# A fused perceiver layer: gather reads first on the SyncE queue, k and v sums ahead of one merged block transpose, maxima over pairs of score banks, and the join of key blocks two at a time

## The chip, the cores and the metric

The kernel runs on one core of one Trainium2 chip. The metric is the device time of one execution in microseconds (us), as the median of several runs.

## The reference, cut to what matters

Sixteen sequences of 128 rows and width 512 pass three sublayers, each with a layer norm before it and a residual sum after it.

```
x = x + xattn(layernorm(x), ctx)   # 16 heads of 32; 2048 context rows per sequence; softmax over them
x = x + mamba_mlp(layernorm(x))    # in_proj, conv, scan over 128 rows with 16 states, out_proj; rmsnorm; MLP of 2048, gelu
x = x + moe(layernorm(x))          # gates by softmax, two largest; a shared and an expert matrix; bias
```

In the attention, k and v are products of the context with weights (512 x 512), scores are q k, and `softmax(scores) v` is made over 2048 context rows.

## The kernel before, in words

**Steps.** Attention is cut into units: a sequence `b` (16), a block `sb` of 512 context rows (4) and a group `hg` of four heads (4), which makes 256 units (`NU`). The loop over `u` (L1329) makes one unit per step; while `u < 256` a step is called live. The scan of the second sublayer runs 54 steps behind (two sequences at a time, 32 steps for a pair), so that from u = 54 to u = 255 both run in one step, and the pattern of a step's other work repeats every 32 steps. After the live steps the MLP and the experts are fed in (L1346); some of that work falls in the last live steps.

**One live step**, in the order in which it is written: loads (L1337 to L1352); four score products into four PSUM banks, one for each head (L307); the weighted sums of the unit before (L386, `weighted`); the reads of the gather (L348, `gathered`); maxima (L315) on DVE; two products for k or v into `pa` and `pc` (L244, `x_products`); four exponentials on ACT (L325); products of dx with B on POOL (L696); the first scan (L731, with L734 and L710); the block transposes (L338, `blocks`); ACT's copy of `pa` (L285, `hold`); k or v sums on DVE (L264, L274, `x_sums`); PE's transposes of two heads (L358) and their copies (L360); the second scan; then the work of the lists `middle`, `late`, `behind`, `after`, `inner`; and last the other products for k or v (`y_products`, L244) with their sums. Every engine runs its own instructions strictly in this written order (`manual_schedule`, L120).

**Two ways to turn probabilities.** The sum over context rows needs the probabilities with these rows on partitions. For the first two heads of a unit PE transposes (L358). For the other two (`ND = 2`) DVE transposes blocks of 32 x 32 (L338), the result is written to DRAM (L342, `trd`) and read back in four pieces in the right order (L348, `pd`). There is one `pd` buffer. The reads for unit u - 1 are issued in step u, behind `weighted`, and used in step u + 1 (L386 with `pd`).

**k and v sums.** k and v are made by a scheme with seven products of quarters, not eight. In steps with phase 1 (u % 4 = 0 and 2) `y_products` adds to `pc` and must wait until `x_sums` has read it. In steps with u % 4 = 3 the product for dt (L663, in list `behind`) writes `pc` and so waits for the v sum too; its result is read by ACT (L667) and DVE (L670).

**Joining key blocks.** Each block of 512 rows has its own maximum and sum. When a sequence is done (e = 16b + 16), `joined`, `joined_first`, `shares`, `joined_second` and `joined_third` make a factor for each block; `spread_out` (L497, POOL) widens it, `scaled` (L503, L508, L510, then L511 on POOL) turns it, multiplies and adds; `attended` (step e + 6, L516) is the output product. In the kernel before, `spread_out` for blocks 0, 1 and 2, 3 is put at e + 2, e + 3, e + 3, e + 4, and `scaled` one step later each.

**Loads.** All these loads go through SyncE's queue, which issues in the written order and waits in place. `load_bc` (L645) brings B (tile `bc0`, used by L696) two steps ahead and C (tile `bc16`, used by L734) one step ahead, each with two buffers. Context (L158) comes four steps ahead. The weights wq (L171), wo (L173), win (L548) and wout (L553) share a ring of six buffers (`WS`); a load into it waits until PE has used the tile that was there. Two of the eight wout tiles are issued inside the product that uses them (`projected`, L760).

**PSUM.** Four score banks, `avp` (weighted sums), `hst` (scan state), `pa` and `pc`. Work in the list `late` takes score banks 2 and 3 while the first two hold the transposes.

Of the kernel before, what the change touches and what calls it, by code (L numbers as in the profile page):

```python
# [15 lines left out]
P = 128  # L16
# [20 lines left out]
def perceiver_layer(ctx: ExitStack, tc: tile.TileContext, a: dict, out: bass.AP):  # L37
# [75 lines left out]
    with ExitStack() as es:  # L113
# [12 lines left out]

        banks = [psum.tile([P, 512], FP, tag=f"s{j}", name=f"bank{j}") for j in range(4)]
        avp = psum.tile([P, 4, P], FP, tag="av", name="avp")  # L130
        hst = psum.tile([P, NH // 2, GT], FP, tag="h0", name="hst")
        pa = psum.tile([P, 2, 256], FP, tag="pa", name="pa")
# [178 lines left out]

        def maxima(u):
            b, sb, hg = split(u)
            for j in range(4):
                nc.vector.tensor_reduce(  # L315
                    stats[b][0][j][:, sb, hg : hg + 1], banks[j], AX.X, ALU.max, negate=True
                )

        def exps(u):
            b, sb, hg = split(u)  # L320
            nm, sm = stats[b]
            pr = pool.tile([P, 4, 512], FP, tag="pr", name=f"pr{u}", bufs=1)
            for j in range(4):
                h = hg * 4 + j
                nc.scalar.activation(  # L325
                    pr[:, j, :],
                    banks[j],
                    AF.Exp,
                    bias=nm[j][:, sb, hg : hg + 1],
                    accum_out=sm[:, sb, h : h + 1],  # L330
                )
            prs[u] = pr

        def blocks(u):

            t = pool.tile([P, 4, ND, 4, 32], FP, tag="tr", name=f"tr{u}", bufs=1)
            for h in range(ND):
                nc.vector.transpose(  # L338
                    t[:, :, h].rearrange("p c i q -> p i c q"),
                    prs[u][:, NP + h, :].rearrange("p (i c k) -> p i c k", i=4, c=4),  # L340
                )
            nc.sync.dma_start(trd[u % 2], t.rearrange("p c h i q -> p (c h i q)"))  # L342

        def gathered(u):
# [70 lines left out]
        def normal(b):  # L415

            x = xts[b]
            root_third(rstd[:, b : b + 1], *xts.pop((b, "r")))
            xn = keep.tile([P, D], FP, tag="aT", name="xn", bufs=1)
            nc.vector.tensor_scalar(  # L420
                xn, x, mv[:, b, 0:1], rstd[:, b : b + 1], ALU.subtract, ALU.mult
            )
            if b:
                nc.gpsimd.tensor_tensor(x, x, bo, ALU.add)
            xts[b, "n"] = xn
            nm = [keep.tile([P, SB, 4], FP, tag=f"nm{j}", name=f"nm{b}_{j}") for j in range(4)]
            sm = keep.tile([P, SB, H], FP, tag="sm", name=f"sm{b}")
            stats[b] = nm, sm

# [31 lines left out]
        def joined(b):  # L461

            parts, sm = stats[b]
            nm = keep.tile([P, SB, H], FP, tag="nm", name=f"nm{b}")
            for j in range(4):
                nc.vector.tensor_copy(
                    nm.rearrange("p s (k j) -> p s k j", j=4)[:, :, :, j], parts[j]
                )
            stats[b] = nm, sm

# [729 lines left out]


        early = {}
        late, after, inner, middle, loads, head, behind, between = ({} for _ in range(8))

        def put(where, u, f):
            where.setdefault(u, []).append(f)
# [1 line left out]
        for b in range(B):  # L1208
            s = 16 * b
            if b:  # L1210
                put(loads, s - 8, lambda b=b: load_x(b))
                put(loads, s - 5, lambda b=b: load_w(0, b))
                put(inner, s - 8, lambda b=b: moments_of(b))
                put(middle, s - 7, lambda b=b: root_of(b))
                put(inner, s - 7, lambda b=b: normal(b))
                put(late, s - 4, lambda ps, b=b: queries(b, ps))
            e = s + 16
            put(loads, e + 5, lambda b=b: load_w(3, b))
            put(inner, e - 1, lambda b=b: joined(b))
            put(inner, e, lambda b=b: joined_first(b))  # L1220
            put(middle, e + 1, lambda b=b: shares(b))
            put(inner, e + 1, lambda b=b: joined_second(b))
            put(head, e + 2, lambda b=b: joined_third(b))
            for sb in range(SB):
                put(inner, e + 2 + (sb + 1) // 2, lambda b=b, sb=sb: spread_out(b, sb))
                put(late, e + 3 + (sb + 1) // 2, lambda ps, b=b, sb=sb: scaled(b, sb, ps))
            put(late, e + 6, lambda ps, b=b: attended(b, ps))
            put(middle, e + 7, lambda b=b: root_of(b))
            put(inner, e + 7, lambda b=b: normed(b))
            put(late, e + 8, lambda ps, b=b: z_turned(b, ps))  # L1230
        for g in range(NG):
            p = 32 * (g + 1)
            for ec in range(EC):
                put(loads, p + 8 + ec, lambda g=g, ec=ec: load_win(g, ec))
                put(loads, p + 8 + ec, lambda g=g, ec=ec: load_win(g, EC + ec))
                put(late, p + 9 + ec, lambda ps, g=g, ec=ec: x_part(g, ec, ps))
                put(late, p + 9 + ec, lambda ps, g=g, ec=ec: z_part(g, ec, ps))
                put(after, p + 10 + ec, lambda g=g, ec=ec: silu_first(g, ec, xas))
                put(after, p + Z_GATES[ec], lambda g=g, ec=ec: silu_first(g, ec, zss))
# [6 lines left out]
                put(between, s - 1 + 4 * ec, lambda g=g, ec=ec: dt_third(g, ec))  # L1246
            for i in range(GB):
                for ec in range(WS):
                    put(loads, s + 32 + 2 * i, lambda g=g, i=i, ec=ec: load_wout(g, i, ec))
                put(loads, s + 31 + 2 * i, lambda b=g * GB + i: reload_x(b))  # L1250
                put(late, s + 33 + 2 * i, lambda ps, g=g, i=i: projected(g, i, ps))

# [76 lines left out]
        for u in range(last):  # L1329
# [4 lines left out]
            made, phase = divmod(u + 3, 4)  # L1334
            makes = 0 < made < B * SB
            of, phase = ("k", "v")[phase // 2], phase % 2
            load_bc(u + 2 - 32 - LAG, 0)  # L1337
            if u % 4 == 1 and made + 1 < B * SB:
                load_ctx(made + 1, ("c00", "c10", "c11"))
            if u % 4 == 2 and made + 1 < B * SB:  # L1340
                load_ctx(made + 1, ("c01",))
            for f in loads.get(u, ()):
                f()
            if scans and u <= NU:
                decays(g, r, 0)
            if u > NU:  # L1346
# [2 lines left out]
                    fed += 1  # L1349
                if scans:  # L1350
                    decays(g, r, 0)
            load_bc(u + 1 - 32 - LAG, DS)  # L1352
            if u == NU + 1:
                load_rows()
            if live:
# [1 line left out]
            if 1 <= u <= NU:  # L1357
# [2 lines left out]
                    weighted_last(u - 2)  # L1360
                weighted_out(u - 1)
                gathered(u - 1)
            for f in early.get(u, ()):
                f()
            if u == NU:
# [25 lines left out]
            silu_third()  # L1391
            if scans:
                scan(g, r, 0)
            if live:
                blocks(u)
            if live and u % 4 == 2:
                values_kept(u // 4)
            if makes:
# [2 lines left out]
                decays(g, r, 1)  # L1401
            if makes:
                x_sums(of, made, phase, pa, pc)

# [8 lines left out]

            ahead = live and u % 16 in (3, 10) and len(after_turns) == 1
            if ahead:
                after_turns[0](banks[3])
                after_turns, places = (), ()
            if live:  # L1420
                for j in range(NP):
# [10 lines left out]
                    f(ps)  # L1432
                    give_back(ps)
            for f in behind.get(u, ()):
                ps = flat(pc) if makes else banks[2] if live else bank()
                f(ps)
                if not live:
                    give_back(ps)
# [84 lines left out]
```

## Time and profile before

| | us |
|---|---|
| median of 3 runs (3809.18 to 3819.37) | 3809.51 |
| the profiled execution | 3817.92 |
| its span, first to last instruction | 3816.1 |
| PE (TensorE) busy | 3602.9 |
| DVE (VectorE) busy | 2862.3 |
| ACT (ScalarE) busy | 2304.2 |
| POOL (GpSimd) busy | 2139.1 |

The groups of instructions that the change touches, from the page's fifth part and the groups by line:

| line, engine | what | count | busy us | mean ns |
|---|---|---|---|---|
| L315 DVE | maxima, 128x512 from PSUM | 1024 | 635.7 | 680 |
| L338 DVE | block transposes, 128x512 | 512 | 338.8 | 696 |
| L325 ACT | exponentials, 128x512 | 1024 | 688.5 | 684 |
| L264 DVE | k sums, 128x256 | 384 | 164.0 | |
| L274 DVE | v sums, 128x512 | 189 | 126.3 | |
| L516 PE | output product of attention | 128 | 65.4 | 659 |

Median time from issue to landing: 5.4 us for `bc`, 3.0 for `trd`, 3.9 for `pd`, 5.7 for wq and wo, 5.2 for win, 4.5 for wout. In all 816.84 MB move, a mean of 214 GB/s.

How to read the views. Busy time is the union of an engine's instructions. The list of waits gives who sat idle, what ended the wait, and three numbers: the total in us, how often, and the longest. A line of the timeline gives start and length in us, engine, line, operation, output and inputs, the count of merged instructions, and in brackets idle time before it with what ended it. "SPq" is SyncE's queue. Matmuls are pipelined and their ends are modelled. An engine's idle time costs something only where that engine holds up the end.

### The profile page before, as it was taken

Reading aid. Unit: us, or ns where it says so; the run is one execution under the profiler, and the core shown is the slowest. Engines: PE = TensorE matmul, PEld = TensorE weight load, DVE = VectorE, ACT = ScalarE, POOL = GpSimd, SP = SyncE. Lnnn points to the kernel's source line nnn. Section 1 sums busy time; section 2 is a strip of 40 time slices with the busy share of each in tenths; the row PEclk is TensorE's granted clock in tenths of the full one; section 3 lists DMA queues with packets and bytes.
Section 4 is the critical chain, followed back from the end, with each engine's and each line's share of the span. In section 5 each row is a group of like instructions: output and inputs, shape, how many; then the busy total and the mean of one; then the engine's idle time right before and its main releaser. Section 6 shows DMA issues by size and latency. Waiting matters only on the chain. (4 is left out here: it accounts for less than half of the span.)

```text
span 3816.1 us, 69166 instructions
## 1 busy us (share of the span) xinstructions
PE 3602.9 (94%) x24072; PEld 2678.4 (70%) x24072; DVE 2862.3 (75%) x5158; ACT 2304.2 (60%) x5672; POOL 2139.1 (56%) x2097
## 2 busy tenths in 40 slices
PE   8999999999899999999999989998999989999999
PEld 6777777777676767677677767686777666655655
DVE  4555557887788778888697878877887777778843
ACT  3555556777566666667576757675766666545431
POOL 2121115676667566767576666666675657577820
PEclk9999999999999999999999999999999999999999
DMA  4444546776777667676766777767776688677752
GB/s 150 145 157 150 158 139 216 223 229 214 243 226 233 206 217 244 217 235 208 241 220 216 221 251 222 235 212 234 238 238 202 214 245 317 208 270 253 242 188 83
DMA packets 527547, 816.84 MB, mean 214 GB/s; under 512 B 44848, under 2 KB 378960, under 8 KB 526944
## 3 DMA queue, kind: packets, MB, share of 16 engines
q1 hardware_dynamic: 526752, 811.79, 66.6%
q8 instruction: 192, 3.15, 0.3%
q14 instruction: 155, 1.27, 0.1%
q0 software_dynamic: 448, 0.63, 0.1%
HBM read 661.51 MB, written 150.73 MB: 213 GB/s over the span
## 5 line engine op out<-in xcount | busy, mean ns | idle before, releaser
L315 DVE TENSOR_REDUCE nm<-bank 128x1 f32<-128x512 f32 x1024 | 635.7, 680 | 221.4 <-PE bank L307 220.2
L747 POOL TENSOR_TENSOR ysum<-ysum,w 128x512 f32<-128x512 f32 x384 | 499.8, 1302 | 515.6 <-DVE hst L710 324.6
L325 ACT ACTIVATE pr<-bank,nm 128x512 f32<-128x512 f32 x1024 | 688.5, 684 | 68.2 <-DVE nm L315 62.1
L696 POOL TENSOR_TENSOR w<-dx,bc 128x512 f32<-128x512 f32 x512 | 651.6, 1294 | 8.9
L731 DVE TENSOR_TENSOR_SCAN hst<-hst,w 128x512 f32<-128x512 f32 x459 | 560.1, 1220 | 43.8 <-ACT hst L717 41.3
L717 ACT ACTIVATE hst<-dt,alog 128x254 f32<-128x254 f32 x918 | 439.9, 479 | 87.5 <-DVE hst L710 67.8
L338 DVE STREAM_TRANSPOSE tr<-pr 128x512 f32<-128x512 f32 x512 | 338.8, 696 | 85.3 <-ACT pr L325 75.9
L386 PEld LDWEIGHTS avp<-pT,v 128*32 128x32 f32 x4096 | 207.7, 112 | 196.2 <-issue 194.2
L734 DVE TENSOR_TENSOR w<-hst,bc 128x512 f32<-128x512 f32 x459 | 317.2, 691 | 19.3 <-DMA bc<-bcd 3.5
L307 PE MATMUL bank<-kt,qT 32*128 32x512 f32 x2048 | 308.6, 641 | 8.1 <-DVE avs L510 5.4
L360 ACT COPY pT<-bank 128x512 f32<-128x512 f32 x512 | 272.0, 582 | 56.1 <-PE bank L358 56.1
L236 POOL TENSOR_TENSOR t<-c,c 128x512 f32<-128x512 f32 x128 | 163.3, 1276 | 229.6 <-PE pc L244 223.9
L386 PE MATMUL avp<-pT,v 128*32 128x128 f32 x4096 | 288.4, 282 | 1.2 <-ACT pT L360 1.1
L386 PE MATMUL avp<-pd,v 128*32 128x128 f32 x3072 | 215.9, 285 | 57.0 <-DMA pd<-trd 57.0
L358 PE MATMUL bank<-ident,pr 128*128 128x128 f32 x2048 | 265.7, 273 | 0.8 <-ACT pr L325 0.7
L358 PEld LDWEIGHTS bank<-ident,pr 128*128 128x128 f32 x2048 | 238.8, 141 | 25.3 <-ACT pr L325 1.8
L244 PE MATMUL pa<-vs,t 128*128 128x256 f32 x1008 | 254.5, 397 | 0.0
L244 PE MATMUL pa<-t,ks 128*128 128x256 f32 x1024 | 249.1, 386 | 0.0
L575 PE MATMUL bank<-zT,win 128*128 128x256 f32 x992 | 224.8, 379 | 0.0
L244 PEld LDWEIGHTS pa<-vs,t 128*128 128x128 f32 x1008 | 192.3, 197 | 38.5 <-issue 12.6
L262 ACT ACTIVATE kt<-pa,bk 128x256 f32<-128x256 f32 x128 | 53.6, 470 | 263.7 <-PE pa L244 263.7
L244 PEld LDWEIGHTS pa<-t,ks 128*128 128x128 f32 x1024 | 186.5, 190 | 36.7 <-issue 14.7
(313 smaller groups left out, 7556.6 us busy)
## 6 DMA issues: line engine op xcount, KB each, us to landing
bc<-bcd SPq DMA_DIRECT2D x512, 512.0 KB, 5.4
trd<-tr SPq DMA_DIRECT2D x256, 512.0 KB, 3.0
pd<-trd SPq DMA_DIRECT2D x1024, 128.0 KB, 3.9
c<-in_ctxT_dram SPq DMA_DIRECT2D x256, 256.0 KB, 5.1
wf<-in_w_dram SPq DMA_DIRECT2D x124, 512.0 KB, 6.5
wqo<-in_wqkvo_dram SPq DMA_DIRECT2D x128, 256.0 KB, 5.7
win<-in_win_dram SPq DMA_DIRECT2D x128, 256.0 KB, 5.2
wout<-in_wout_dram SPq DMA_DIRECT2D x128, 256.0 KB, 4.5
```

The costliest lines, as they stand in the source:

```text
L244: nc.tensor.matmul(ps[:, r, :], l[:, kc, r * P : (r + 1) * P], m[:, kc, :], start=(i in (1, 2, 5) and r == 0 and kc == 0), stop=(r == 1 an ...
L307: nc.tensor.matmul(banks[j], qts[b][rows, hg, :], kts[u // 4, hg][rows, :], start=True, stop=True)
L315: nc.vector.tensor_reduce(stats[b][0][j][:, sb, hg : hg + 1], banks[j], AX.X, ALU.max, negate=True)
L325: nc.scalar.activation(pr[:, j, :], banks[j], AF.Exp, bias=nm[j][:, sb, hg : hg + 1], accum_out=sm[:, sb, h : h + 1],)
L338: nc.vector.transpose(t[:, :, h].rearrange("p c i q -> p i c q"), prs[u][:, NP + h, :].rearrange("p (i c k) -> p i c k", i=4, c=4),)
L358: nc.tensor.transpose(ps[:, i, :], prs[u][:, j, i * P : (i + 1) * P], ident)
L386: nc.tensor.matmul(avp[j * HD : (j + 1) * HD, v % 4, :], values(v, i, j), pts[v, j][:, i, :] if j < NP else pds[v][:, :, j - NP, i, :], st ...
L696: nc.gpsimd.tensor_tensor(w, dx.unsqueeze(1).to_broadcast([P, NH // 2, GT]), bcs[g * 32 + r, 0][:, i * NH // 2 : (i + 1) * NH // 2, :], AL ...
L717: nc.scalar.activation(bt(h[:, k, :])[:, :, 1:], bt(dt)[:, :, 1:], AF.Exp, scale=aneg[:, ec, n : n + 1],)
L731: nc.vector.tensor_tensor_scan(flat, flat, w.rearrange("p n t -> p (n t)"), 0.0, ALU.mult, ALU.add)
L734: nc.vector.tensor_tensor(w, h, bcs[g * 32 + r, DS][:, i * NH // 2 : (i + 1) * NH // 2, :], ALU.mult)
L747: nc.gpsimd.tensor_tensor(s, s, w, ALU.add)
```

## The change

Six edits in the live steps:

- The loads of a live step (except u = 0) move from the head of the step to a place behind the reads of the gather. Within them the order becomes: the other loads, `bc0`, `bc16`, context.
- The loads of wq, wo, win and wout form a list of their own, `weights`. In live steps they are issued behind `blocks` and its write; later they go with the other loads.
- `blocks` moves behind `x_sums` and makes one transpose instruction for both heads.
- The four score banks become two tiles of two banks each. One reduction gives the negated maxima of two banks; what joins them afterwards makes two copies in place of four.
- `spread_out` for the four blocks goes to e + 2, e + 2, e + 3, e + 3, with `scaled` one step later.
- dt's product takes a free score bank (2 or 3) where `late` leaves one; the piece of late work that is done ahead of PE's transposes takes bank 2 in place of bank 3.

```diff
-        banks = [psum.tile([P, 512], FP, tag=f"s{j}", name=f"bank{j}") for j in range(4)]
+        pairs = [psum.tile([P, 2, 512], FP, tag=f"s{m}", name=f"bank{m}") for m in range(2)]
+        banks = [pairs[j // 2][:, j % 2, :] for j in range(4)]
...
-            for j in range(4):
+            for m in range(2):
                 nc.vector.tensor_reduce(
-                    stats[b][0][j][:, sb, hg : hg + 1], banks[j], AX.X, ALU.max, negate=True
+                    stats[b][0][m][:, sb, hg, :], pairs[m], AX.X, ALU.max, negate=True
                 )
...
-                    bias=nm[j][:, sb, hg : hg + 1],
+                    bias=nm[j // 2][:, sb, hg, j % 2 : j % 2 + 1],
...
-            for h in range(ND):
-                nc.vector.transpose(
-                    t[:, :, h].rearrange("p c i q -> p i c q"),
-                    prs[u][:, NP + h, :].rearrange("p (i c k) -> p i c k", i=4, c=4),
-                )
+            nc.vector.transpose(
+                t.rearrange("p c h i q -> p (h i) c q"),
+                prs[u][:, NP:, :].rearrange("p h (i c k) -> p (h i) c k", i=4, c=4),
+            )
...
-            for j in range(4):
+            for m in range(2):
                 nc.vector.tensor_copy(
-                    nm.rearrange("p s (k j) -> p s k j", j=4)[:, :, :, j], parts[j]
+                    nm.rearrange("p s (k m j) -> p s k m j", m=2, j=2)[:, :, :, m, :], parts[m]
                 )
...
-                put(loads, s - 5, lambda b=b: load_w(0, b))
+                put(weights, s - 5, lambda b=b: load_w(0, b))
...
-            put(loads, e + 5, lambda b=b: load_w(3, b))
+            put(weights, e + 5, lambda b=b: load_w(3, b))
...
-                put(inner, e + 2 + (sb + 1) // 2, lambda b=b, sb=sb: spread_out(b, sb))
-                put(late, e + 3 + (sb + 1) // 2, lambda ps, b=b, sb=sb: scaled(b, sb, ps))
+                put(inner, e + 2 + sb // 2, lambda b=b, sb=sb: spread_out(b, sb))
+                put(late, e + 3 + sb // 2, lambda ps, b=b, sb=sb: scaled(b, sb, ps))
...
-                put(loads, p + 8 + ec, lambda g=g, ec=ec: load_win(g, ec))
-                put(loads, p + 8 + ec, lambda g=g, ec=ec: load_win(g, EC + ec))
+                put(weights, p + 8 + ec, lambda g=g, ec=ec: load_win(g, ec))
+                put(weights, p + 8 + ec, lambda g=g, ec=ec: load_win(g, EC + ec))
...
-                    put(loads, s + 32 + 2 * i, lambda g=g, i=i, ec=ec: load_wout(g, i, ec))
+                    put(weights, s + 32 + 2 * i, lambda g=g, i=i, ec=ec: load_wout(g, i, ec))
...
-            load_bc(u + 2 - 32 - LAG, 0)
-            if u % 4 == 1 and made + 1 < B * SB:
-                load_ctx(made + 1, ("c00", "c10", "c11"))
-            if u % 4 == 2 and made + 1 < B * SB:
-                load_ctx(made + 1, ("c01",))
-            for f in loads.get(u, ()):
-                f()
+
+            def step_loads():
+                for f in loads.get(u, ()):
+                    f()
+                for f in weights.get(u, ()) if u > NU else ():
+                    f()
+                load_bc(u + 2 - 32 - LAG, 0)
+                load_bc(u + 1 - 32 - LAG, DS)
+                if u % 4 == 1 and made + 1 < B * SB:
+                    load_ctx(made + 1, ("c00", "c10", "c11"))
+                if u % 4 == 2 and made + 1 < B * SB:
+                    load_ctx(made + 1, ("c01",))
+
+            if not 1 <= u <= NU:
+                step_loads()
...
-            load_bc(u + 1 - 32 - LAG, DS)
...
                 gathered(u - 1)
+                step_loads()
...
-            if live:
-                blocks(u)
             if live and u % 4 == 2:
                 values_kept(u // 4)
...
                 x_sums(of, made, phase, pa, pc)
+            if live:
+                blocks(u)
+            for f in weights.get(u, ()) if u <= NU else ():
+                f()
...
-                after_turns[0](banks[3])
+                after_turns[0](free[0])
...
-                ps = flat(pc) if makes else banks[2] if live else bank()
+                n = len(late.get(u, ()))
+                if live and n < len(free):
+                    ps = free[n]
+                else:
+                    ps = flat(pc) if makes else banks[2] if live else bank()
```

## The prediction

> **What bounds the kernel now.** I read the page's first part, then the table of 100 us stretches, then TensorE's waits, then the SyncE queue's own waits, then one step of the timeline. The first part:
>
> ```profile
> PE 3602.9 (94%) x24072; PEld 2678.4 (70%) x24072; DVE 2862.3 (75%) x5158; ACT 2304.2 (60%) x5672; POOL 2139.1 (56%) x2097
> ```
>
> The reader is to see that TensorE (PE) is idle for only 3816.1 - 3602.9 = 213 us, so nothing that keeps PE's work as it is can gain more. The table of stretches says where: the 26 stretches from 600 to 3200 us, in which attention and scan run together, hold 180 us of it. PE's waits name it:
>
> ```profile
> PE avp L386 <- DMA pd<-trd: 65.1, 21, 4.8
> PE bank L516 <- POOL aT L511: 34.0, 13, 2.8
> PE pc L244 <- DVE kt L264: 30.5, 25, 2.5
> PE pc L663 <- DVE v L274: 22.9, 32, 0.9
> PE pc L244 <- DVE v L274: 12.9, 24, 1.0
> PE bank L307 <- DVE avs L510: 5.4, 12, 0.5
> ```
>
> (us in total, times, longest.) Six waits, 170.8 us, most of the idle time; each is met by one part of the change. The first is the gather of the transposed probabilities. It takes 3.9 us from issue to landing (the page's sixth part) and a step lasts 8 to 24 us, so it is late only where its issue is. The SyncE queue says why:
>
> ```profile
> SPq L548 <- PE avp L443: 87.1, 14, 12.7
> SPq L548 <- PE bank L575: 81.1, 8, 11.6
> SPq L553 <- PE bank L516: 48.5, 24, 6.5
> ```
>
> Weight loads (L548, L553) stand in the queue ahead of the gather and wait up to 12.7 us for a buffer that PE frees late in the same step. Third, one step of the timeline (start us, length us):
>
> ```profile
> 1511.13 1.04 PE L358 MATMUL bank<-ident,pr 128*128 128x128 f32 x8
> ...
> 1511.20 1.31 DVE L338 STREAM_TRANSPOSE tr<-pr 128x512 f32<-128x512 f32 x2
> ...
> 1512.43 0.83 DVE L264 SCALAR_TENSOR_TENSOR kt<-pc,bk,u1k 128x256 f32<-128x256 f32 x2
> ...
> 1513.32 1.99 PE L244 MATMUL pc<-c,ks 128*128 128x256 f32 x8 [1.15 <-DVE kt L264]
> ```
>
> PE has ended its transposes at 1512.17 and waits 1.15 us for sums that VectorE (DVE) runs behind its own two transposes.
>
> **The change, part by part.** All against the profiled execution, 3817.9 us (span 3816.1 and 1.8 around it).
>
> *Reads first, weights last.* In a live step the four reads of the gather now precede the step's other loads, and the loads of wq, wo, win and wout go behind the write of the blocks. The gather waits only for PE's weighted sums of that step, which end 2.2 us after its first score product (1505.50 to 1507.7), is issued in about 1.7 us (four issues, 1507.71 for 1.76) and lands 3.9 us later: about 8 us into a step, needed 1.1 us into the next one, so just in time in the shortest steps (8.3 us) and early elsewhere. Of 65.1 us one wait of 4.8 (the last gather, needed in its own step) stays, and I leave 3 for the short steps: **-57**.
>
> What is late next: everything the gather is put ahead of. The two bc loads of a step left the queue at about -1 and +1.2 us (1504.56 and 1506.73); now they leave at about +4. Matched by order over the steps, the first has 6 to 20 us from landing to its product on GpSimd (L696), the second mostly 7 to 17 to L734. The shift takes 4 to 10 us of the first, 3 to 8 of the second, and up to 2.4 us more (512 KB at the mean 214 GB/s) if they queue behind the gather's bytes. In most steps 1 to 5 us remain; I put **+5** for those in which they don't. [...]
>
> The weight loads leave some 9 to 12 us later than before. wo lands 12.6 to 16 us ahead of use now (step 16b+6), wq at u%32 = 28 some 14.3, win 12 to 20: all stay ahead, wq by about 0.5 us only; **+5** there (0 to 20: seven times 3). At u%32 = 25 the last two wout tiles (L553) are issued inside the product that uses them, behind the write of the blocks; the sixth product starts 5.2 us in, and they land 4.2 to 7.2 us in now. With that write 0.5 to 1.5 us later and bc and three context loads newly in front, I take 2 us each, seven times: **+13** (0 to 20).
>
> *Blocks joined in two and two.* The two last factors of a batch are spread and multiplied a step earlier, so the last GpSimd addition (L511, 1.27 us) has a whole step before the output product (L516) needs it: 34.0 becomes about 1, **-33**. The same products and copies are made; the 5.4 us of L307 behind L510 move to other steps and stay.
>
> *Sums ahead of the block transpose.* k and v sums no longer wait behind 1.31 us of transposes. In the step above they would start at 1511.2, end at 1512.03, and PE would not wait. What is next there is ACT's copy of pa (L285), which ends behind the fourth exponential, and PE's own transposes. Of 30.5 + 12.9 I leave 10 for steps in which DVE is already behind (u%32 = 2, 2.5 us of wait): **-33**. The transposes and the write of the blocks end about 0.8 us later; the gather that reads them waits for PE anyway, so that is covered but for the shortest steps. If that cover went, each 0.8 us in a third of the 202 steps would cost 54 us.
>
> *dt in a free bank.* L663 waited for v only because it wrote pc. It now takes a score bank where one is free (u%32 = 7, 23, 27, 31), and where it keeps pc the sums are earlier. But the next scores then wait for DVE to have read dt out of that bank (L670, 0.47 us, behind the second scan): in the step at 1880.41 that reading would end at about 1890.3, and PE would want the bank at about 1889.8. So 22.9 becomes about 8: **-15**.
>
> *Maxima of two banks at once, one merged transpose.* 1024 reductions of 680 ns (635.7 us busy) become 512 of twice the elements. No row shows that shape. A tiny operation on DVE takes 154 ns (L94), so 512 elements take about 530, and 1024 would take 1.21 us. The ends are 1.0 and 1.36 (two old ones): DVE gains 512 x (1.24 - 1.21), some 16 us, between a loss of 61 and a gain of 124. The transposes, 512 of 696 ns, become 256 of about 1.2 (1.1 to 1.4): some 30 us less, between -20 and +57. The copies that join the maxima (L466) halve. All this is on DVE, beside PE: I cost it at nothing by itself. The first exponential starts about 0.5 us later, since the pair is released as one; PE's transposes start 5.6 us into the step and the second exponential ended 1.9 us ahead of them (1509.2 to 1511.13), which hides it. Without that cover it would cost 0.5 us in each of 256 steps, 128 us.
>
> **The sum.** -57 - 33 - 33 - 15 = -138; +5 + 5 + 13 = +23; together -115, so 3817.9 becomes 3702.9. The profiled execution was 8.4 us above the median of the runs (3809.51), so the forecast for the median is 3694. About 0.3%, 11 us, is what a measurement here can tell from no change.
>
> **Rivals.**
>
> 1. *New waits take half.* For it: every cover above is 0.5 to 3 us wide and the steps get shorter, DVE is 91 to 92% busy in the densest stretches (1300-1400, 2500-2600 us), and 1850-1860 has the DMA engines fully busy. Against: those stretches have almost no PE idle time now. If wq and wout cost 40, dt and the sums keep 25 more: -138 + 40 + 5 + 25 = -68, 3742.
>
> 2. *No new wait shows.* All of 170.8 but the 4.8 and 5.4: -160, 3649. Against: wout at u%32 = 25 waits even now (3.0 us, three times).
>
> 3. *Same.* The gather is still late, now for its semaphores or the later write, and the sums are held by L285: -138 shrinks to nothing, 3799 to 3821. Against: the timeline, where L285 ended at 1511.12, before DVE's transposes began.
>
> 4. *Slower.* The second bc load, now behind the gather, lands after the scan's product needs it in every step; DVE runs in order, so maxima, exponentials and PE's transposes all shift. Price: d us in each of 202 steps. It decides from d = 138/202 = 0.7 us beyond a slack of 1 to 5 us; at d = 1 the time is 3809.5 - 138 + 202 = 3874. For it: SyncE needs 0.4 to 0.7 us an issue, seven or more of them in a row. Against: three quarters of the steps keep over 2 us.
>
> **Chances.** Forecast (3660 to 3725) 0.55; rival 1 (3725 to 3798) 0.24; rival 2 (below 3660) 0.07; rival 3 0.05; rival 4 0.09. Faster 0.55 + 0.24 + 0.07 = 0.86. The range takes in the ends of the unknown costs of the forecast and most of rival 1: 3650 to 3775 leaves out about 0.2.
>
> **What would show it.** PE's waits for pd, aT, kt and v should almost be gone from its list, PE's busy time stay at about 3603, and its idle time fall to about 98. DVE's maxima should be 512 of about 1.21 us. New entries to look for: L516, L443 or L760 behind a load of weights, L307 behind L670, DVE's L734 behind bc. If DVE's share stays under 80% and the idle time is not smaller, the queue order is where I am wrong; if PE's busy time grows, my bound was wrong, since matmul ends in this profile are modelled.

## The result, and the profile after

| | median, us | ratio to before, 95% interval |
|---|---|---|
| before (4 runs, 3809.18 to 3819.60) | 3814.44 | |
| the changed kernel (4 runs, 4344.87 to 4361.72) | 4355.13 | 1.1415 [1.1381, 1.1449] |

The forecast was 3694, so the direction was wrong and the time lies 661 us off. The profiled execution has a span of 4359.7 us, 544 more than before. From here on lines are those of the kernel shown: in the changed kernel they lie up to two further than before (scores L308, PE's transposes of two heads, called turns, L358, their copies L360, block products of `scaled` L505, in_proj L577, wout L762), and between the experiments they differ by up to four.

The first part and the groups of the page of the changed kernel (busy us, mean ns of one, then idle time ahead of them and its main releaser):

```profile
PE 3714.8 (85%) x24072; PEld 2706.1 (62%) x24072; DVE 2817.6 (65%) x4358; ACT 2312.4 (53%) x5672; POOL 2135.4 (49%) x2097
...
L316 DVE TENSOR_REDUCE nm<-bank 128x2 f32<-128x1024 f32 x512 | 602.5, 1218 | 336.2 <-PE bank L308 336.0
...
L358 PE MATMUL bank<-ident,pr 128*128 128x128 f32 x2048 | 325.3, 282 | 315.0 <-ACT pT L360 312.6
...
L338 DVE STREAM_TRANSPOSE tr<-pr 128x1024 f32<-128x1024 f32 x256 | 316.0, 1234 | 3.6 <-ACT pr L326 2.1
```

DVE did what was forecast: a maximum over two banks takes 1218 ns (estimate 1.21 us), the merged transpose 1234 ns. But PE, idle for 213 us before, is now idle for 4359.7 - 3714.8 = 645 us, and it is busy for 112 us more with the same 24072 instructions. PE's waits (us in total, times, longest):

```profile
PE bank L358 <- ACT pT L360: 312.6, 256, 3.5
PE bank L577 <- issue: 132.0, 58, 3.9
PE bank L762 <- DMA wout<-in_wout_dram: 40.7, 12, 5.3
PE bank L505 <- DVE avs L512: 31.4, 15, 2.4
PE bank L505 <- DVE aT L510: 29.8, 16, 2.4
...
PE avp L386 <- DMA pd<-trd: 4.4, 2, 4.0
```

The waits for aT at the output product, for v at dt's product and for the k and v sums are gone from the list and `pd` fell from 65.1 to 4.4, all as forecast. In their place stands a wait that happens 256 times, once in each unit, and that the prediction doesn't name: PE's transposes wait for ACT's copy. One such step of the timeline (start us, length us, what, and in brackets the idle time before it):

```profile
2142.27 0.60 PE L358 MATMUL bank<-ident,pr 128*128 128x128 f32 x4
...
2143.25 0.58 ACT L360 COPY pT<-bank 128x512 f32<-128x512 f32 x1
...
2143.88 0.66 PE L358 MATMUL bank<-ident,pr 128*128 128x128 f32 x4 [1.01 <-ACT pT L360]
...
2144.57 0.58 ACT L360 COPY pT<-bank 128x512 f32<-128x512 f32 x1 [0.75 <-PE bank L358]
```

Before, the eight transposes of the two heads were one stream of 1.04 us. Now head 0's four are made (0.60), ACT copies them out (until 2143.83), and only then may head 1's four begin, though they go to another bank. Both banks now belong to one tile. The program orders PE's writing of the second half of the tile behind the reading of the first, because that is how they stand in the code. The two in_proj products show the same at L577:

```profile
1850.07 1.89 PE L577 MATMUL bank<-zT,win 128*128 128x256 f32 x8
...
1852.01 0.56 ACT L587 ACTIVATE xa<-bank,convb,convw 128x256 f32<-128x256 f32 x1 [0.81 <-PE bank L577]
1852.60 1.51 DVE L592 SCALAR_TENSOR_TENSOR xa<-bank,convw,xa 128x254 f32<-128x254 f32 x3 [0.43 <-ACT xa L587]
...
1854.21 1.97 PE L577 MATMUL bank<-zT,win 128*128 128x256 f32 x8 [2.25 <-issue]
```

The product for z, in bank 3, waits until ACT and DVE have read the product for x out of bank 2 (ends 1854.11). The view names "issue" as releaser; the times of the readers' ends name the real one.

**Where the theories stood after this.** Theory T: the tile of two banks is the loss, and the rest of the change gains what was forecast. Rivals: the merged reduction itself delays the step (theory R); or the new order of SyncE (SP) does (theory Q). SP's own queue gave reason for the last: it stood 806.3 us for the landing of the blocks' write, and 81.1 us before. First the kernel before, then the changed one:

```profile
SPq L348 <- DMA trd<-tr: 81.1, 68, 3.6
```

```profile
SPq L348 <- DMA trd<-tr: 806.3, 228, 9.3
```

### The profile page after: what moved, and what is told of

Its sections match the earlier page's. It is cut to its first block, busy times and chain, and to the rows that moved or that the text cites. A ratio compares the mean times of both kernels' runs of the same rounds, so it can differ in the third digit from the quotient of the medians.

```text
span 4359.7 us, 68304 instructions
## 1 busy us (share of the span) xinstructions
PE 3714.8 (85%) x24072; PEld 2706.1 (62%) x24072; DVE 2817.6 (65%) x4358; ACT 2312.4 (53%) x5672; POOL 2135.4 (49%) x2097
## 3 DMA queue, kind: packets, MB, share of 16 engines
q14 instruction: 148, 1.21, 0.1%
## 5 line engine op out<-in xcount | busy, mean ns | idle before, releaser
L316 DVE TENSOR_REDUCE nm<-bank 128x2 f32<-128x1024 f32 x512 | 602.5, 1218 | 336.2 <-PE bank L308 336.0
L358 PE MATMUL bank<-ident,pr 128*128 128x128 f32 x2048 | 325.3, 282 | 315.0 <-ACT pT L360 312.6
L358 PEld LDWEIGHTS bank<-ident,pr 128*128 128x128 f32 x2048 | 236.8, 142 | 401.9 <-ACT pT L360 373.3
L360 ACT COPY pT<-bank 128x512 f32<-128x512 f32 x512 | 297.4, 581 | 222.9 <-PE bank L358 222.9
L577 PE MATMUL bank<-zT,win 128*128 128x256 f32 x992 | 258.7, 408 | 132.1 <-issue 132.0
L338 DVE STREAM_TRANSPOSE tr<-pr 128x1024 f32<-128x1024 f32 x256 | 316.0, 1234 | 3.6 <-ACT pr L326 2.1
L577 PEld LDWEIGHTS bank<-zT,win 128*128 128x128 f32 x992 | 189.9, 201 | 178.9 <-issue 155.0
L308 PE MATMUL bank<-kt,qT 32*128 32x512 f32 x2048 | 297.4, 643 | 2.0 <-ACT pT L360 2.0
L386 PE MATMUL avp<-pT,v 128*32 128x128 f32 x4096 | 275.4, 277 | 0.0
L245 PE MATMUL pa<-vs,t 128*128 128x256 f32 x1008 | 261.6, 405 | 0.0
L245 PE MATMUL pa<-t,ks 128*128 128x256 f32 x1024 | 255.4, 393 | 0.0
L625 POOL TENSOR_TENSOR xa<-xa,sg 128x256 f32<-128x256 f32 x64 | 46.5, 726 | 370.5 <-ACT sg L624 184.4
L245 PEld LDWEIGHTS pa<-vs,t 128*128 128x128 f32 x1008 | 197.9, 202 | 40.2 <-issue 10.3
L245 PEld LDWEIGHTS pa<-t,ks 128*128 128x128 f32 x1024 | 192.2, 196 | 41.2 <-issue 17.6
```

The lines of the kernel that those rows point to most:

```text
L245: nc.tensor.matmul(ps[:, r, :], l[:, kc, r * P : (r + 1) * P], m[:, kc, :], start=(i in (1, 2, 5) and r == 0 and kc == 0), stop=(r == 1 an ...
L316: nc.vector.tensor_reduce(stats[b][0][m][:, sb, hg, :], pairs[m], AX.X, ALU.max, negate=True)
L338: nc.vector.transpose(t.rearrange("p c h i q -> p (h i) c q"), prs[u][:, NP:, :].rearrange("p h (i c k) -> p (h i) c k", i=4, c=4),)
L358: nc.tensor.transpose(ps[:, i, :], prs[u][:, j, i * P : (i + 1) * P], ident)
L386: nc.tensor.matmul(avp[j * HD : (j + 1) * HD, v % 4, :], values(v, i, j), pts[v, j][:, i, :] if j < NP else pds[v][:, :, j - NP, i, :], st ...
L577: nc.tensor.matmul(ps, w[:, kc, :], zTs[g][:, kc, :], start=(kc == 0), stop=(kc == KC - 1))
```

## The experiments

Each kernel was timed beside the kernel before on the same chip, and its ratio is to that.

### The tile of two banks

**e1_four_tiles**: the changed kernel with four tiles of one bank and four maxima, all else kept.

```
-pairs = [psum.tile([P, 2, 512], FP, tag=f"s{m}", ...) for m in range(2)]
-banks = [pairs[j // 2][:, j % 2, :] for j in range(4)]
+banks = [psum.tile([P, 512], FP, tag=f"s{j}", name=f"bank{j}") for j in range(4)]
```

> The changed kernel with the score banks as four tiles of one bank and four maxima again; all else of the change kept. Theory T (a tile of two banks is guarded as one: PE may not write one bank while ACT or DVE still has to read the other) expects the waits of L358 behind the copy (312.6 us), of the second late product (132 us) and of the two block products (61 us) to vanish, and the half-clock stretches with them: 3690 us, 3650 to 3740. Theory Q (the loads behind the reads make the loss) expects no less than 4250.

**e2_tiles_alone**: the opposite edit in the kernel before, two tiles of two banks, with the four maxima left as they were.

> The kernel before with its score banks as two tiles of two banks, and nothing else; four maxima of one bank each. Theory T expects the new waits here too, with no merged instruction at all: 256 waits of about 1.2 us of L358 and about 2.2 us for each second late product, 3814 plus 300 to 600, so 4110 to 4410. Theory Q, and a theory R by which the reduction over two banks is what holds the banks, expect 3814 within 10.

Measured: e1 3812.88, ratio 0.9987 [0.9975, 1.0000]; e2 4302.65, ratio 1.1269 [1.1244, 1.1295]. Taking the pair tile out, together with the merged maxima, gives back 4355 - 3813 = 542 us; putting the tile alone into the kernel before costs 4303 - 3818 = 485. PE's waits of e2, whose maxima are not merged:

```profile
PE bank L359 <- ACT pT L361: 301.2, 256, 2.6
PE bank L576 <- issue: 125.9, 56, 2.3
```

These are the two new waits of the changed kernel. So theory T holds for the loss: the tile alone, without the merged reduction, makes nearly all of it. But e1 should have reached 3690 and stands at the time of before: the second half of theory T fell, and what follows below is about that.

**e3_turns_first**: the changed kernel with both heads' transposes written ahead of both copies. **e4_crossed**: heads 0, 2 and 1, 3 share a tile, so that the two heads that PE turns lie in different tiles; merged maxima kept.

> The changed kernel with PE's transposes of both heads written ahead of both copies, so that no copy of the pair stands between them in the written order. Theory T expects the wait of L358 behind the copy (312.6 us) to go and the others to stay: 3960 us, 3880 to 4050. Theories Q and R expect 4355 within 30.

> The changed kernel with heads 0 and 2 in one tile and heads 1 and 3 in the other, so that the two transposes, and the two late products, write different tiles; the maxima stay merged over two banks. Theory T expects most of the new waits to go: 3720 us, 3660 to 3800, with 512 maxima of 1.22 us. Theory R (the merged reduction) and theory Q expect at least 4200.

Measured: e3 4273.26, ratio 1.1202 [1.1180, 1.1225]; e4 4102.56, ratio 1.0754 [1.0729, 1.0779]. Both expectations missed. In e3 the wait of the transposes for copies is gone, but the other pairs that share a tile still wait, now longer:

```profile
PE bank L579 <- issue: 176.5, 58, 4.2
PE bank L764 <- DMA wout<-in_wout_dram: 62.9, 12, 7.7
PE bank L507 <- DVE aT L512: 55.3, 16, 5.0
PE bank L507 <- DVE avs L514: 50.8, 15, 3.8
```

In e4 the work in the free banks 2 and 3 shares tiles with the heads that are being copied, and waits for these copies:

```profile
PE bank L577 <- ACT pT L360: 58.5, 49, 1.6
...
PE bank L505 <- ACT pT L360: 28.9, 27, 2.1
PE bank L665 <- ACT pT L360: 25.1, 21, 1.7
```

Neither of the two pairings that were run leaves the work beside it unbound: 312.6 us of waiting at the turns in the changed kernel, 58.5, 28.9 and 25.1 us behind the copies in e4. In e3 PE's idle time falls by only 132 us (645 to 513), and its busy time grows by 43 (3714.8 to 3757.8), with the granted clock at half for 474 us in place of 337. How e3's and e4's remaining loss splits between the named waits and what follows them was not told apart.

### Reads first

**p1_reads_first**: the kernel before with the reads of the gather ahead of all the step's other loads, and nothing else of the change. The weights stay among these loads; that they go behind the write, the second half of this part, is left out.

```
+                gathered(u - 1)
+                step_loads()      # loads (weights too), bc, bc, ctx: at the head of the step before
```

**e5_weights_early**: e1 with the weight loads at the end of `step_loads`, ahead of the blocks' write. **c2_weights_ahead**: e1 with them at the head of the step, ahead of the reads.

> The kernel before with the step's loads, the weights among them, behind the reads of the gather, and nothing else. By the prediction's term the wait for pd falls from 65 to about 8 and 5 us come back: 3815 - 52 = 3763, 3745 to 3785. Rival X expects 3805 or more.

> The run with four one-bank tiles, but with the weight loads issued at the end of the step's other loads (behind the reads, ahead of the write of the blocks) in place of behind that write. Theory W (weights behind the write give back what the rest gains: 67 us of waits for wout, 25 for wq and wo, and part of the 19 for pd) expects 3720 us, 3680 to 3755, with those waits under 20 us in all. Rival X (the gain is lost whatever the place of the weights, to transfers that collide or to DVE) expects 3790 or more.

> The four-tile form of the changed kernel, with its weight loads issued at the head of the step, ahead of the four reads, where the kernel before has them. Theory Q: SP waits there for the blocks' landing anyway, so the loads take time that was lost; the waits for wout and wq/wo (87 us) fall to under 15 and the half clock with them: 3813 to 3735 (3710 to 3765). Rival (any load put between write and read stretches the write's landing and so moves the wait on): the wait for pd rises by as much as wout falls, 3790 to 3840.

Measured: p1 3964.42, ratio 1.0403 [1.0383, 1.0423]; e5 3891.40, 1.0206 [1.0191, 1.0221]; c2 3874.15, 1.0153 [1.0128, 1.0178]. All three lie above what the theory said, p1 with the wrong sign: without the weights behind the write, the part that was to gain 57 us costs 150 alone. The rivals of p1 and e5 (3805 or more, 3790 or more) held; c2 lies above its rival's 3840 too. PE's waits of p1, then SP's:

```profile
PE bank L760 <- DMA wout<-in_wout_dram: 100.0, 12, 10.1
PE pc L244 <- DVE kt L264: 69.5, 35, 6.1
...
PE avp L386 <- DMA pd<-trd: 9.2, 7, 3.0
```

```profile
SPq L348 <- DMA trd<-tr: 1486.2, 243, 10.2
SPq L348 <- PE avp L386: 181.4, 63, 6.7
```

`pd` is early now, 9.2 for 65.1. But a read can't be issued before the write that it reads has landed, and that write is the last thing that SP issued in the step before. With the reads at the head of the step SP stands for it, 6.1 us each time (1486.2 / 243), and all loads wait behind. They then go out in one bunch just ahead of the next write, and the median time to its landing goes from 3.0 us to 7.4 (the page's sixth part; 6.3 in e1). If it is the bunch that delays it, which the order suggests and no run shows by itself, the loss feeds itself. What comes late with it is bc too: POOL waits 274.5 us and DVE 150.8 us for it, where before DVE waits 3.5 and POOL is not in the list. DVE also waits longer before it refills `tr`, which the late write still reads (it has one buffer): 83.1 us, and 8.5 before. PE's longer wait for the k sums (69.5 for 30.5) follows mostly from this second wait: 13 of its 35 cases, 41.6 us, come within 5 us of it, and 8.1 us come behind a wait for bc. The largest waits of DVE in p1:

```profile
DVE nm L315 <- PE bank L307: 205.2, 145, 2.9
DVE xn L769 <- PE bank L760: 154.1, 13, 13.6
DVE w L734 <- DMA bc<-bcd: 150.8, 79, 6.5
DVE tr L338 <- DMA trd<-tr: 83.1, 65, 4.9
```

Weights put earlier (e5, c2) make it worse: SP stood 1337.5 and 1060.5 us for the write, against 951.2 in e1, DVE waits 42.5 and 81.4 us for bc, against 33.3, and the wait for wout that they were to remove is 119.0 and 75.4 us, against 63.5. With the weights behind the write, and beside the other parts, the early reads cost next to nothing: 3811 us without them (c1 below), 3813 with them (e1).

**h1_old_blocks** takes the standing away: e1 with four buffers for the blocks and with reads that fetch the blocks of one step earlier, so heads 2 and 3 are weighted with another step's probabilities and its output is not the layer's; only its time is of use.

```
-trd[u % 2].rearrange(...)
+trd[max(u - 1, 0) % 4].rearrange(...)
```

> The four-tile form of the changed kernel, with four buffers for the blocks in DRAM, where the reads take the blocks of the step before the one that they should: so heads 2 and 3 are weighted with the wrong step's probabilities, all shapes and counts kept. SP then has no landing to wait for. Theory Q: SP's wait for the write (951 us) goes, the loads behind the reads are issued up to 6 us earlier, wout 67 and wq/wo 25 fall to under 20 together: 3700 (3670 to 3740), what was predicted for the whole change. Rival (the loads are late because the DMA engines are full, not because SP stands): the waits for wout stay above 50 and the time above 3780.

Measured: 3745.52, ratio 0.9819 [0.9802, 0.9836]: 67 us below e1. SP no longer stands for the write, PE waits 1.4 us for `pd` and DVE 1.3 us for bc. The size was missed: `wout` still costs 56 us.

```profile
PE bank L759 <- DMA wout<-in_wout_dram: 56.3, 12, 7.0
PE pc L244 <- DVE kt L264: 17.3, 20, 2.3
PE bank L515 <- DMA wqo<-in_wqkvo_dram: 13.7, 17, 2.2
```

Matched by order, the trace shows why: the last two wout tiles, issued inside the product, leave SP 1.7 to 6.0 us after its start instead of 1.1 and 1.9, and land 8.1 to 12.9 us in, where before it was 3.7 to 7.8 (12 products in live steps). The six other wout tiles now stand just ahead of them; whether SP's time to issue or the bytes in front weigh more was not told apart.

### The other parts alone and together

**p2_sums_first**, **p3_join** and **p4_dt_bank** are single parts put into the kernel before (p2 with the merged transpose; p3 `(sb + 1) // 2` to `sb // 2` in both lines; p4 with `free[n]` for dt and bank 2 for the piece ahead of the turns). **c1_no_reads_first** is all three, **c3_sums_join** the first two, **e6_dt_as_before** is e1 with dt's product put back.

> The kernel before with the sums ahead of one merged transpose, and nothing else. By the prediction's term -33 us, and up to 15 more since dt's product waits for the same sums: 3775, 3760 to 3795; the transposes 256 of 1.23 us. Rival X expects 3805 or more, with the wait for pd grown by what the sums lose, since the write of the blocks comes later.

> The kernel before with the key blocks joined in two and two, and nothing else. By the prediction's term -33 us: 3782, 3770 to 3795, the wait of the output product behind the last addition gone. Rival X expects 3805 or more.

> The kernel before with one part alone: dt's product in a free bank of the heads where there is one, in place of the bank of k's and v's sums. The wait of L663 for v's sums (22.9 us, 32 times) goes but for few, as does half of what follows: 3800 (3790 to 3812) by the prediction's term; 3814 (3808 to 3820) if the end of the wait is only passed on to the turns behind.

> The kernel before with three of the parts: sums ahead of one merged transpose, blocks joined two and two, dt's product in a free bank of the heads; SP's order and the four one-bank tiles stay as before. Theory Q (the reads put first make SP wait for the landing of the write just ahead of them, and every load behind them goes late): the parts add, -20 and -40 as measured alone and -5 to -15 for the bank, from 3814: 3745 (3725 to 3765), below every kernel so far; pd is still waited for some 65 us, wout 3. Rival (the parts gain only together with early reads, because the wait for pd takes over what they free): 3780 or more, with pd's waits at 90 or more.

> The kernel before with sums ahead of one merged transpose and blocks joined two and two, nothing else. Theory S (dt's product in a free bank splits the four heads' scores of the next step into two pairs, +0.8 us in 51 steps, and that ate the gain of the three parts together): without it 3770 (3755 to 3785), the line of the scores at 309 or 317 us again. Rival (the wait for pd takes over whatever the other parts free): 3800 (3790 to 3815), pd above 100.

> The four-tile form of the changed kernel with dt's product back in the bank of k's and v's sums. Theory S: the scores fall from 345 to 300 us, dt's wait for v's sums comes back by at most 5 us since the sums now come first: 3813 to 3770 (3750 to 3785). Rival (the split is only where the wait for dt shows, and moves to the product itself): 3805 to 3820.

| kernel | median, us | ratio, 95% interval | PE's wait for pd, us |
|---|---|---|---|
| before | 3813.64 to 3817.57 | | 65.1 |
| p2 sums first | 3794.43 | 0.9948 [0.9930, 0.9967] | 80.7 |
| p3 join | 3774.30 | 0.9909 [0.9889, 0.9928] | 80.9 |
| p4 dt in a free bank | 3821.55 | 1.0009 [0.9994, 1.0024] | 67.6 |
| c3 sums and join | 3800.44 | 0.9960 [0.9946, 0.9974] | 117.8 |
| c1 sums, join, dt | 3811.39 | 0.9993 [0.9978, 1.0008] | 112.5 |
| e1 all, with reads first | 3812.88 | 0.9987 [0.9975, 1.0000] | 19.3 |
| e6 as e1, dt as before | 3808.23 | 0.9982 [0.9970, 0.9994] | 26.9 |

p2 and p3 came within their ranges, p4 at 3822 above both of its own. In c1, c3 and e6 the time is the rival's. The join and the sums gain 40 and 20 us alone and 13 together: the wait for `pd` takes over most of what they free (65.1 before, 81 in each alone, 118 together), and PE's busy time is 17 us longer in c3 than before (3620.1 for 3602.9). One line of c3 holds most of what PE waits for in its live steps:

```profile
PE avp L385 <- DMA pd<-trd: 117.8, 44, 5.4
```

And dt's product in a free bank gains nothing, though its wait of 22.9 us does go. Before, the four heads' scores of a step run at once: eight products of 0.64 us each (median, form 32*128) take 1.14 us together. In e1, behind a step with dt, two of the heads wait for DVE to read dt:

```profile
810.85 1.14 PE L307 MATMUL bank<-kt,qT 32*128 32x512 f32 x8
```

```profile
801.46 1.13 PE L307 MATMUL bank<-kt,qT 32*128 32x512 f32 x4
802.87 1.13 PE L307 MATMUL bank<-kt,qT 32*128 32x512 f32 x4 [0.29 <-DVE dt L669]
```

The first fence is the kernel before, the second e1. The timeline shows 0.29 us of waiting; the cost is 2.54 us (801.46 to 804.00) for 1.14, since each half stream takes as long (1.13 us) as the whole. In p4 the 51 steps behind dt take a mean of 1.91 us for their scores (1.14 before), 39 us in all, of which 36 stand as busy time: L307 344.2 for 308.6. That eats the 22.9.

### Which loads have to stand ahead

**c4_bc_ahead**: c3 with ctx, x and weight loads behind the reads, but both bc loads left ahead of them.

```
 load_bc(u + 2 - 32 - LAG, 0)
-if u % 4 == 1 ...: load_ctx(...)       # and the list `loads`
...
 load_bc(u + 1 - 32 - LAG, DS)
...
 gathered(u - 1)
+step_loads()                           # ctx, then the list `loads`
```

**c5_ctx_behind**: only ctx behind. **c6_wout_ahead**: as c4, wout back at the head of the step. **c7_bc_ahead_dt_bank**: c4 with dt in a free bank.

> Sums and join as in c3, and the ctx, x and weight loads of a step put behind the four reads, while the two bc loads stay ahead of them. Theory Q: the bc loads fill the time in which the blocks' write lands, so SP stands little there (130 us to at most 400), pd's wait falls from some 80 to 25, wout's rises to at most 25: 3730 (3700 to 3765). Rival (any load behind the reads comes late through the standing SP): wout above 50, 3790 or more.

> As c4, but only the ctx loads are put behind the reads; weights and x stay ahead. Theory Q: pd's wait falls to 50, wout's stays under 10: 3745 (3720 to 3770). Rival: SP stands as in reads first (above 700 us for the write) and the time is 3790 or more.

> As c4, with wout's loads (six tiles in each of 14 steps) back at the head of their steps, ahead of the reads. Theory Q with a full queue: 1.5 MB ahead of the reads put them some 6 us back in these steps, so pd is waited for by 3 to 4 us in 12 of them (+40) and wout's 44 fall to 15: no gain, 3700 (3685 to 3720). Rival (only the standing SP makes wout late, the reads don't mind six loads): 3660 (3645 to 3675).

> As c4, with dt's product in a free bank of the heads, the part of the change that c4 leaves out. Theory S: the scores of 51 steps run in two pairs of heads, 0.8 us longer each, the scores' line goes from 321 to 355 us; no wait for v's sums is left to be saved: 3694 to 3727 (3710 to 3740). Rival (the split only fills time that the next step would wait anyway): 3694 (3685 to 3702).

| kernel | median, us | ratio, 95% interval | SP stands for the write | PE waits: pd, wout (into a bank) |
|---|---|---|---|---|
| c3 (all loads ahead) | 3800.44 | 0.9960 [0.9946, 0.9974] | 129.4 | 117.8, 1.2 |
| c5 (ctx behind) | 3780.51 | 0.9913 [0.9895, 0.9930] | 228.0 | 104.8, 0.4 |
| **c4 (all but bc behind)** | **3694.21** | **0.9688 [0.9671, 0.9704]** | 428.2 | 7.5, 44.3 |
| c6 (c4, wout ahead) | 3698.26 | 0.9693 [0.9675, 0.9712] | 400.0 | 43.0, 1.2 |
| c7 (c4, dt in a free bank) | 3705.34 | 0.9713 [0.9696, 0.9730] | 419.9 | 6.6, 47.1 |

c4 beats both kernels: 3.1% below before, 15% below the changed one, and faster than its expected 3700 to 3765, though its wait for wout (44.3) is longer than the 25 expected. That its median equals the forecast for the whole change is chance, since it is another kernel. The page of c4 and its waits:

```profile
PE 3572.6 (97%) x24072; PEld 2660.7 (72%) x24072; DVE 2845.0 (77%) x4902; ACT 2303.5 (62%) x5672; POOL 2140.9 (58%) x2097
```

```profile
PE bank L759 <- DMA wout<-in_wout_dram: 44.3, 12, 5.1
PE pc L244 <- DVE kt L264: 16.5, 20, 2.3
PE pc L244 <- DVE v L274: 8.4, 17, 0.9
PE avp L385 <- DMA pd<-trd: 7.5, 5, 5.8
```

The two bc loads are issued while the write lands; DVE waits 4.7 us for them and POOL does not, and the loads behind the reads no longer delay the reads. From the issue of a write to the issue of its reads, a mean over steps 60 to 254 matched by order in the trace, the time is 8.2 us before, 7.1 in c3, 6.2 in c4 and 8.6 in p1: with everything behind them the reads go out *later* than with everything ahead. Of the 106 us from c3 to c4, ctx alone gives 20 (c5 missed, at 3780); the rest comes only when the weight and x loads move as well. These without ctx, and c4's order without the sums and the join, were not run. c6 met its expectation: what wout wins, `pd` loses. c7 came out between the two theories: 11 us above c4, and its scores' line at 342.0 us (c4 320.6). The two intervals overlap a little, but c1 over c3 (+11, intervals apart), p4 over before (+6) and e1 over e6 (+5), the last two within their uncertainty, have the same sign.

## Why the prediction was wrong

- **"Maxima of two banks at once": "I cost it at nothing by itself."** This step failed, by some 540 us. The edit was priced by what the new instructions cost on DVE (right to 1%), not by what the new *tile* binds. The prediction even saw that "the pair is released as one", and applied it to the first exponential alone; the same holds for every later use of these banks: turns, x and z products, scaled factors. The turns alone wait 1.22 us in each of 256 steps (312.6 / 256). The waits in this program go by tile, and e2 shows their price when a tile has two banks: 4303 us for 3818.
- **"PE's busy time stay at about 3603"**: it grew by 112 us. Two sources show. The eight transposes, 1.04 us as one stream, take 0.60 + 0.66 as two: 256 x 0.22 = 56 us (L358: 265.7 to 325.3). And the granted clock is at half for 337 us instead of 152, which makes an estimated 185 / 2 = 93 at most, if PE's work takes twice as long there: eight products of L245 took 3.62 us at half clock (1092.51) and 1.99 at full (1082.26). How the 112 split between them was not measured.
- **"Reads first ... -57"**: the term for `pd` itself was nearly right (65.1 to 19.3 in e1, 9.2 in p1). Two sentences failed. "The gather waits only for PE's weighted sums" left out the landing of the write ahead of it: SP stood 1486 us in p1 and 951 in e1. And "+5" and "+13" for the loads behind took the loads as moved by the length of four issues; they are moved by the standing as well. Wout's waits of 67 us in e1 (5 before) stand for 13 more that were forecast, wq's and wo's 25 (2.5 before) for 5 more. The prediction allowed for bc queued behind the bytes of the reads (up to 2.4 us), but not for the write behind bc, where the traces show 3.0 us to landing before and 7.4 in p1.
- **"Blocks joined in two and two, -33"**: right in the mechanism; -40 alone, and the wait for aT is gone. The size has some luck in it: of the waits that went (34.0 for aT, 5.4 at L307), 16 us came back on `pd`, and PE's busy time fell by 20 (3602.9 to 3582.5, with the clock at half for 119 us in place of 152), which no term held.
- **"Sums ahead of the block transpose, -33"**: the mechanism was right, the size not: -20. The waits of `pc` fell from 43.4 to 21.7 (10 were left in the sum), PE's busy time grew by 21 (3602.9 to 3624.2), and `pd` took 16 more. The cover that the prediction named ("the gather that reads them waits for PE anyway") got thinner: SP's wait for PE ahead of the reads fell from 441.8 to 248.1 us, that for the write's landing rose from 81.1 to 120.6. Whether the later write makes the 16 is open: p3, which leaves it in place, shows 16 as well.
- **"dt in a free bank, -15"**: no gain; +5 to +11 in four pairs of runs, of which only c1 over c3 is clear of the noise. The prediction saw the wait for DVE's reading, but not that a short wait in the middle of the four heads' scores splits one stream of 1.14 us into two of 1.13.
- **The sum** added the parts. Measured without the tile and the queue order, -40 and -20 make -13 (c3): the waits behave as links of a loop in which the slowest (blocks, write, reads) sets the pace when the others are gone. c4 shortens that link (6.2 us from write to reads for 7.1 in c3) and reaches -119.
- **Rival 4** (bc late, DVE in order, PE behind it) did not make the loss: bc is late in p1 (150.8 us of DVE's waiting) and less so in e1 (33.3), but behind a *standing* SP, not behind four issues. Even in p1 only some 15 us of PE's waits for the k and v sums (69.5 and 20.2) stand behind a wait for bc. In the changed kernel DVE's wait is 5.2 us; there the loss is PE behind its own tile, which no rival named.

## What to carry to other kernels

Before two buffers are merged so that one instruction can read both, list every other user of either half: where the program's waits go by tile, each write to one half will wait for reads of the other, and the merged instruction must pay for all of it. In a queue that waits in place, don't ask only what a moved transfer waits for now, but what it will have to wait for at its new place, and put work there that would have been issued anyway. Gains from waits in one loop don't add: measure the parts together, and look at which wait grew.

## What the runs showed of the hardware

**Half the clock after short gaps.** In the changed kernel the clock record shows 70 stretches at half clock, of 3.41 us or twice or three times that (the last is cut at 2.67), 337 us in all (before: 31, 152 us). One of them by windows (length, PE, PEld, DVE, ACT and POOL busy, granted clock, DMA share, GB/s):

```profile
1083.00:1089.30 6.30, 4.51 (x26) 3.63 (x24) 5.66 (x8) 5.13 (x14) 1.96 (x2) 1.00 0.79 250
1089.30:1096.10 6.80, 5.32 (x18) 3.99 (x18) 2.46 (x5) 0.89 (x2) 4.69 (x6) 0.50 0.19 77
1096.10:1102.00 5.90, 5.90 (x60) 4.48 (x60) 4.25 (x5) 5.14 (x15) 2.21 (x3) 1.00 0.39 120
```

The half clock starts at 1089.33, 0.6 us into a wait of 2.05 us and 1.7 us behind the end of one of 1.22 us. In the 8 us ahead of 51 of 69 such stretches no single gap reaches 3 us, and in 40 the longest is 2.0 to 2.5, in 30 of these with another of 0.8 to 1.6 us. In this record the changes of the clock lie on a grid of 3.413 us, and counted by its windows the case is clearer: in each of the 69 windows just ahead of a half-clock stretch PE was idle for 53% or more of the 3.413 us (here 1.82 us, the least of them), and in none of the 1107 windows at full clock that full clock followed was it idle for more than 59%. So in this run a large idle share of a window went ahead of the half clock. In the kernel before it is looser: of the 31 windows just ahead of such a stretch two have an idle share below 53% (1.28 of 3.41 us from 45.00, 1.69 from 1038.28). What brings the half clock about was not shown; no run was made for it.

**One DVE instruction of doubled size cost a little less than two here**: 1218 ns for 1024 elements against two times 680 in the maxima, 1234 against two times 696 in the block transposes, some 10% less.
